# First pair of an attention-and-adapter kernel: x's mean on four column tiles, and another order of the preparation of W

## The chip, the cores and the metric

One core of one Trainium2 chip runs the whole program. The metric is the device time of one execution in microseconds (us). The engines are named PE (TensorE, matrix products), DVE (VectorE), ACT (ScalarE), POOL (GpSimd) and SP (SyncE, which here only issues DMAs).

## The reference, cut to what matters

```python
# x: (128, 128, 1024) f32, adj: (128, 128, 128) int32, W: (1, 1024, 1024), a: (1, 16, 128, 1)
h  = layernorm(x)                                    # no scale, no offset
Wh = h @ W                                           # split in 16 heads of 64
e  = leaky_relu(Wh @ a[:, :64] + Wh @ a[:, 64:], 0.2)    # one score a row and head
att = softmax(where(adj == 0, -9e15, e)) * adj
x  = x + elu(att @ Wh)
y  = layernorm(x)
gates = top-2 softmax of y[:, 0] @ router.T          # 8 experts of rank 16
x  = x + y + sum over e of gates[e] * (y @ down_e.T) @ up_e.T
```

There are 128 tiles of 128 rows and 1024 columns. W and the router, down and up tables are the same for all of them.

## The kernel before, in words

The layernorm is not applied to x. Since a row's mean drops out when W's columns have their mean taken away, the kernel centres W's columns (over the 1024 rows of W) and multiplies the product by the row's rstd afterwards. Wh's scores come out of the same product, as four extra columns beside each 256 columns of W ("score columns"), which are W times a.

Tiles are worked on in pairs q = 0 to 63. The product of two tiles with W is done as a Strassen-like scheme of seven half-sized products on blocks of W: B11, B21, B22 and the fourth block of W (loaded into the place called T1) give T3 = B22 - (fourth block), T2 = T3 + B11, T1 = B22 - T2 (which replaces the fourth block) and NT4 = B21 - T2. On x's side POOL forms four sums (`pair_sums`). Each product is 8 matmuls of 128 x 256 (260 with score columns), 16 PE instructions in the profile, since each f32 matmul shows as two. Three banks of PSUM accumulate: x (products 1 and 2), y (6, 5, 3) and z (7, 4). There are buffers for two of them at a time, so z takes the place of x once x has been read, last by DVE's `low(q, 0)`.

The order of every engine's queue is the order in which the program is written. A list `gaps` holds eight lists for each q: the work to be issued before product 1 (gap 0), between the products, and after the last one (gap 7). For q = 0 the products run in the order 1, 2, 7, 6, 5, 3, 4; for the others 1, 6, 2, 5, 7, 3, 4. Reads of a product by DVE (u2 after 6, u4 after 5, wh0 after 3, wh1 after 4) are queued where the product is issued, ahead of the next gap's work.

In the first pair W is not yet prepared, and `prepare(gaps)` spreads that work over pair 0:

- `center_x` takes the column mean from x of pair 0, so that its products 1 and 2 may use W as loaded. PE sums over 128 partitions with a matrix of 1/1024 (`mean_of`, L180), DVE subtracts (L183).
- `partial_means(h)` sums one half of W's columns, on four column tiles of PE (L191: four matmuls with 32 output rows each run side by side); ACT copies the result (L195), `column_means` (L200) adds the four parts with `sum_of` into a tile w_mean, of which `center_block` (L209) takes each block's mean away. `combine` (L746) forms T3, T2, T1 and NT4. Each is one DVE instruction over 2048 elements a partition.
- `first_stats(i)` (L306, L307 on DVE, L310 and L311 on POOL for rstd), `first_half` (L754) and `correct_p1` (L761) bring product 1's result in line with the centred W.
- `score_rows` (PE, L220) forms a times W's transpose, `center_rows` (DVE L229 to L232, ACT L235) takes its mean away, `turn_rows` (PE L244) transposes it, and `score_columns` (DVE L254 to L259) puts it beside the blocks. From pair 1 on, products read these columns.
- For pair 0 itself the scores are had another way: `score_of(b)` multiplies by a on POOL (L270), and DVE sums by head (L204).
- `high` (ACT, L442) and `low` (DVE, L446) write the attention's operands in two parts, `attention_weights` (DVE L462 to L479) the softmax, `attend` (PE L488) the product with adj, `update` (DVE L498, L506, L507, ACT L505) x + elu. `turn` and `rejoin` transpose x by DMA for the logits.
- `experts()` (L277 to L300) takes the mean off the router and down tables over their 1024 rows: for each of the two a DVE sum over 8 chunks (L281), a PE sum over partitions (L283) and a DVE subtraction (L284); then a store of the down table to DRAM (L285, SP), which later pairs gather from, and small index tables. It is issued once, in pair 1.

SP issues at the start, in this order: a, x of pair 0 transposed (1 MB), B11, B21, the two tiles of x, B22, the fourth block (about 1 MB each), W transposed (4 MB), adj, the next pair's x. SP's queue and POOL's DMA queue are in order too.

Of the kernel before, what the change touches and what calls it, by code (L numbers as in the profile page):

```python
# [8 lines left out]
F32 = mybir.dt.float32  # L9
# [5 lines left out]
ALU = mybir.AluOpType  # L15
AX = mybir.AxisListType
# [9 lines left out]
def adj_ffn_kernel(  # L26
# [16 lines left out]
    nc = tc.nc  # L43
    B, N, D = x.shape
    P = 128
    KC = D // P
    KH = KC // 2
    F = 64
    H = D // F
    ER = up_t.shape[0]  # L50
    E = router_t.shape[2]
# [3 lines left out]
    HALF = 512  # L55
# [10 lines left out]
    work = ctx.enter_context(tc.tile_pool(name="work", bufs=2))  # L66
    small = ctx.enter_context(tc.tile_pool(name="small", bufs=3))
    ps_w = ctx.enter_context(tc.tile_pool(name="ps_w", bufs=2, space=bass.MemoryType.PSUM))
    ps_m = ctx.enter_context(tc.tile_pool(name="ps_m", bufs=4, space=bass.MemoryType.PSUM))
# [7 lines left out]
    GRP = {}  # L77
# [7 lines left out]
    B11, B21, B22, T1, T2, T3, NT4 = range(7)  # L85
# [25 lines left out]
    def w_at(h, k):  # L111

        return w_sb[:, BLOCK[h][k // KH], k % KH]
# [52 lines left out]
    def spread_a():  # L166

        for h in range(NH):
# [2 lines left out]
                             start=True, stop=True)  # L171
            nc.scalar.copy(a_sum[:, h], in_two(pa))

    def center_x():

        xt = XT[0]
        px = ps_m.tile([P, HALF], F32, tag="pm", name="px")[:, 0:2 * P]
        mean = px.rearrange("p (t n) -> p t n", t=2)
        for k in range(KC):
            nc.tensor.matmul(mean, mean_of, xt[:, :, k], start=(k == 0), stop=(k == KC - 1))  # L180
        for t, lo, hi in ((0, 0, KH), (0, KH, KC), (1, 0, KC)):
            part = xt[:, t, lo:hi]
            nc.vector.tensor_tensor(part, part, mean[:, t, None].to_broadcast(part.shape),  # L183
                                    ALU.subtract)

    def partial_means(h):

        pc = ps_m.tile([P, HALF], F32, tag="pm", name="pc")
        for u in range(2):
            for c in range(KH):  # L190
                nc.tensor.matmul(pc[c * 32:(c + 1) * 32], mean_of[:, 0:32],  # L191
                                 w_sb[:, BLOCK[h][u], c, :, MAIN], start=(u == 0), stop=(u == 1),
                                 tile_position=(0, c * 32))
        part = work.tile([P, HALF], F32, tag="hp", name="part")
        nc.scalar.copy(part, pc)  # L195
        return part

    def column_means(part):
        pc = ps_m.tile([P, HALF], F32, tag="pm", name="w_mean")
# [62 lines left out]
    def score_of(b):  # L262
# [7 lines left out]
        nc.gpsimd.tensor_tensor(prod, src, a_sum[:, h], ALU.mult)  # L270
        by_head(dst, prod)

    slot = down_row = up_row = None

    def experts():

        nonlocal slot, down_row, up_row  # L277
        down_rows = down_sb.rearrange("p e r k -> p (e r) k")
        for t, n in ((router_sb.rearrange("p k e -> p e k"), E), (down_rows, ER)):
            sums = work.tile([P, ER], F32, tag="hp", name="sums")  # L280
            nc.vector.tensor_reduce(sums[:, 0:n], t, AX.X, ALU.add)  # L281
            pr = ps_m.tile([P, HALF], F32, tag="pm", name="pr")[:, 0:n]
            nc.tensor.matmul(pr, mean_of, sums[:, 0:n], start=True, stop=True)  # L283
            nc.vector.tensor_tensor(t, t, pr[:, :, None].to_broadcast([P, n, KC]), ALU.subtract)  # L284
        nc.sync.dma_start(table.rearrange("(e p) c -> p e c", p=P),  # L285
                          down_sb.rearrange("p e r k -> p e (r k)"))

# [479 lines left out]
    def prepare(gaps):  # L767

        got = {}

        def keep(name, f, *of):
            def task():
                got[name] = f(*(got.get(o, o) for o in of))
            return (task,)

        gaps[0] += [(place_a,), (spread_a,), (center_x,), (pair_sums, 0)]
        gaps[2] += [keep("part 0", partial_means, 0), (first_stats, 0),
                    keep("less", first_half), (first_stats, 1),
                    keep("", column_means, "part 0"), (keep_c11,), (high, 0, 0),
                    (combine, T3, B22, T1, ALU.subtract)]  # L780
        gaps[3] += [keep("part 1", partial_means, 1), (center_block, 0, B11),
                    keep("", correct_p1, "less"), (combine, T2, T3, B11, ALU.add), (center_block, 0, B21)]
        gaps[4] += [keep("", column_means, "part 1"), keep("rows", score_rows), (score_of, 0),
                    (center_block, 1, B22), (combine, T1, B22, T2, ALU.subtract),
                    keep("turned", center_rows, "rows")]
        gaps[5] += [(combine, NT4, B21, T2, ALU.subtract), (load_experts,)]
        gaps[6] += [keep("cols", turn_rows, "turned"), (score_of, 3)]
        gaps[7] += [keep("", score_columns, "cols"), (score_of, 1)]

    NQ = B // 2  # L790

# [1 line left out]
    for q in range(NQ + 2):  # L793
# [27 lines left out]
                gaps[3].insert(0, (turn_at_end, i + 1))  # L821
            gaps[5] += [(join, i), (join, i + 1)]
        if q + 1 < NQ:
            gaps[3 if q else 6].append((first_stats, 2 * q + 2))
            gaps[4 if q else 6] += [(pair_sums, q + 1), (first_stats, 2 * q + 3)]
        if q == NQ - 1:
            gaps[1].append((load_all,))
            gaps[5].append((order_all,))
# [15 lines left out]
                gaps[5].append((load_adj, q // 2 + 1))  # L844
        if q < NQ:
            gaps[3].insert(0, (low, q, 0))
            gaps[6] += [(low, q, 3), (low, q, 1)]

        if q + 1 < NQ:
            load_xt(q + 1)  # L850
            load_x(q + 1)
        if q == 0:
            gaps[7].append((score_of, 2))
        if q == 1:
            gaps[6].append((experts,))
        products = project(q) if q < NQ else iter(())
        for gap in gaps:
            for f, *args in gap:
# [48 lines left out]
```

## Time and profile before

| | |
|---|---|
| median of 3 runs | 1970.37 us (1970.11 to 1972.25) |
| the profiled execution | 1969.22 us, of which the profile's span is 1967.4 us |
| PE busy | 1936.3 us, 98% of the span |
| DVE busy | 1657.0 us, 84% |
| ACT / POOL busy | 1080.0 us, 55% / 835.3 us, 42% |
| mean granted PE clock | 0.994 |
| products (L373) on the chain that ended last | 77% of the span |

A row of a timeline gives the start, the length and the engine of a group of instructions on one line of the kernel, what it writes and reads, the shape of one, their number, and in brackets the time for which the engine was idle before them with what ended it. A row of busy time by stretch gives the stretch and its length, then for each engine (PE, PE's weight loads, DVE, ACT, POOL) its busy time and number of instructions, then PE's granted clock, and the share and GB/s of the DMA engines. Where PE alone is asked for, the row has PE alone. A clock of 0.50 is half speed. The records of the clock begin in this trace at 12.21 us; before that the stretches show 1.00, while matmuls of 256 columns stand 0.427 us apart there, against 0.216 later.

### The profile page before, as it was taken

What the parts mean: (1) busy time and instruction counts of PE and PEld (TensorE: products, weight loads), DVE (VectorE), ACT (ScalarE), POOL (GpSimd) and SP (SyncE); (2) the same over time, 40 slices, a digit from 0 to 9 for tenths busy, and PEclk for the clock granted to TensorE, in tenths of its full rate; (3) what the DMA queues carried; (4) which work ended last, traced back from release to release, by engine and by line L of the source; (5) the groups of instructions that cost most, each with busy time, mean ns of one, the idle gap of its engine ahead of it and who ended that gap; (6) DMA issues with size and microseconds to landing.
All of it is one profiled execution on the core that took longest, in us unless ns stands there. A gap on an engine that the chain in (4) does not pass through costs nothing.

```text
span 1967.4 us, 30167 instructions
## 1 busy us (share of the span) xinstructions
PE 1936.3 (98%) x11042; PEld 1576.6 (80%) x11042; DVE 1657.0 (84%) x3511; ACT 1080.0 (55%) x1031; POOL 835.3 (42%) x1123
## 2 busy tenths in 40 slices
PE   8799999999999999999999999999999999999997
PEld 5688888888888888888888888888888888888885
DVE  6788888888888888888888888888888888888886
ACT  1355655655555655655655655655655655555653
POOL 2344344544335544435534435534435534435530
PEclk9899999999999999999999999999999999999999
DMA  7365566565566565566566565565565565565552
GB/s 280 86 161 171 153 188 182 129 195 169 153 185 178 130 197 173 151 186 174 137 193 176 150 188 167 144 193 176 151 188 159 152 193 169 159 187 150 161 154 104
DMA packets 343671, 329.26 MB, mean 167 GB/s; under 512 B 274274, under 2 KB 276322, under 8 KB 342884
## 3 DMA queue, kind: packets, MB, share of 16 engines
q1 hardware_dynamic: 325940, 285.37, 49.4%
q0 software_dynamic: 17008, 40.91, 7.0%
q8 instruction: 88, 1.44, 0.3%
q10 hardware_dynamic: 576, 1.05, 0.1%
q14 instruction: 59, 0.48, 0.1%
HBM read 193.58 MB, written 67.63 MB: 133 GB/s over the span
## 4 chain that ended last, share of the span: by engine, by line
PE 92%; DVE 4%; DMA 1%; ACT 1%; issue 1%; POOL 0%; SPq 0%; POOLq 0%; DVEq 0%
PE pw L373 77%; PE ph L488 6%; PE pu L677 3%; PE pd L661 3%; DMA tt<-halves 1%; PE pb L624 1%; PE pl L568 1%; DVE stats L306 1%; ACT y_t L544 1%; DVE xn L506 1%; DVE xn L507 1%; DVE hp L498 0%; ACT halves L538 0%; PE pu L738 0%; DVE w_sb L746 0%
## 5 line engine op out<-in xcount | busy, mean ns | idle before, releaser
L373 PE MATMUL pw<-w_sb,xt 128*128 128x260 f32 (+1 forms) x4096 | 951.8, 387 | 7.0 <-issue 5.6
L373 PEld LDWEIGHTS pw<-w_sb,xt 128*128 128x128 f32 x4096 | 770.5, 191 | 154.3 <-issue 34.4
L373 PE MATMUL pw<-w_sb,s 128*128 128x260 f32 (+1 forms) x3072 | 711.1, 385 | 2.9 <-DVE w_sb L746 2.0
L373 PEld LDWEIGHTS pw<-w_sb,s 128*128 128x128 f32 x3072 | 578.0, 190 | 117.1 <-issue 21.0
L310 POOL TENSOR_SCALAR rstd<-mv 128x2 f32<-128x2 f32 x128 | 30.4, 238 | 862.7 <-DVE mv L307 857.4
L544 ACT COPY y_t<-tt 128x2048 uint16<-128x2048 uint16 x126 | 315.8, 2509 | 77.0 <-DMA tt<-halves 76.6
L306 DVE BATCH_NORM_STATS2 stats<-xn 128x6 f32<-128x512 f32 x512 | 324.0, 675 | 0.1
L642 POOL DMA_INDIRECT down<-table,at_down x248 | 252.0, 1016 | 163.7 <-DVE e L462 89.3
L538 ACT COPY halves<-xn 128x2048 uint16<-128x2048 uint16 x126 | 239.7, 1902 | 120.6 <-DVE xn L507 76.9
L442 ACT ACTIVATE parts<-wh,rstd 128x512 fp32r<-128x512 f32 x192 | 133.6, 715 | 224.9 <-DVE wh L381 224.6
L505 ACT ACTIVATE ex<-hp 128x1024 f32<-128x1024 f32 x128 | 135.4, 1058 | 179.3 <-DVE hp L498 177.6
L681 DVE SCALAR_TENSOR_TENSOR xn<-pu,rstd,xn 128x512 f32<-128x512 f32 x248 | 169.0, 745 | 21.8 <-PE pu L677 21.8
L498 DVE TENSOR_TENSOR hp<-ph,att 128x512 f32<-128x512 f32 x256 | 161.4, 672 | 10.6 <-PE ph L488 10.1
L507 DVE SCALAR_TENSOR_TENSOR xn<-ex,xn 128x1024 f32<-128x1024 f32 x128 | 156.8, 1225 | 13.7 <-issue 0.5
L488 PE MATMUL ph<-parts,adj_f 128*128 128x512 f32 x512 | 164.2, 442 | 1.3 <-ACT parts L442 0.9
L506 DVE SCALAR_TENSOR_TENSOR xn<-hp,xn 128x1024 f32<-128x1024 f32 x128 | 156.8, 1225 | 4.4
L560 ACT ACTIVATE xn<-xn,off,mul 128x1024 f32<-128x1024 f32 x128 | 151.2, 1230 | 0.7 <-POOL off L525 0.7
L446 DVE SCALAR_TENSOR_TENSOR parts<-wh,rstd,parts 128x512 fp32r<-128x512 f32 x192 | 139.1, 752 | 12.4 <-ACT parts L442 12.4
L381 DVE TENSOR_TENSOR wh<-pw,u 128x520 f32<-128x520 f32 (+1 forms) x128 | 89.3, 698 | 54.7 <-PE pw L373 51.3
L381 DVE TENSOR_TENSOR wh<-pw,p 128x520 f32<-128x520 f32 (+1 forms) x64 | 44.8, 700 | 81.4 <-PE pw L373 81.4
L488 PEld LDWEIGHTS ph<-parts,adj_f 128*128 128x128 f32 x512 | 96.5, 189 | 20.3 <-ACT parts L442 1.2
L311 POOL TENSOR_TENSOR rstd<-rstd,half_pow 128x2 f32<-128x2 f32 x128 | 91.3, 713 | 10.7
(138 smaller groups left out, 1473.5 us busy)
## 6 DMA issues: line engine op xcount, KB each, us to landing
xt<-in_x_t SPq DMA_DIRECT2D x128, 512.0 KB
xn<-in_x SPq DMA_DIRECT2D x128, 512.0 KB
out_y<-xn SPq DMA_DIRECT2D x124, 512.0 KB
adj_f<-in_adj_t POOLq DMA_DIRECT2D x32, 256.0 KB
adj_i<-in_adj SPq DMA_DIRECT2D x32, 256.0 KB
w_sb<-in_w SPq DMA_DIRECT2D x4, 1040.0 KB
down<-table,at_down POOLq DMA_INDIRECT x248
wt_sb<-in_w_t SPq DMA_DIRECT2D x1, 2048.0 KB
```

What stands on the lines that cost most here:

```text
L306: nc.vector.bn_stats(st[:, h, :], X[i][:, h * HALF:(h + 1) * HALF])
L373: nc.tensor.matmul(dst[:, j, cols], lhs[:, k, :], w_sb[:, rhs, k, j, cols], start=(first and k == 0), stop=(k == KH - 1), skip_group_check ...
L446: nc.vector.scalar_tensor_tensor(in_two(PARTS[q][:, 1, b]), block, rstd, in_two(PARTS[q][:, 0, b].bitcast(F32)), op0=ALU.mult, op1=ALU.sub ...
L488: nc.tensor.matmul(PH[i][h], GRP[g]["adj_f"][:, t, :], PARTS[q][:, s, NH * (i % 2) + h], start=(s == 0), stop=(s == 1))
L498: nc.vector.tensor_tensor(hp[:, h * HALF:(h + 1) * HALF].rearrange("p (h f) -> p h f", f=F), ph.rearrange("p (h f) -> p h f", f=F), att[:, ...
L506: nc.vector.scalar_tensor_tensor(xt, hp, 0.0, xt, op0=ALU.max, op1=ALU.add)
L507: nc.vector.scalar_tensor_tensor(xt, ex, 1.0, xt, op0=ALU.min, op1=ALU.add)
L538: nc.scalar.copy(halves, X[i].bitcast(U16).rearrange("p (d s) -> p s d", s=2))
L544: nc.scalar.copy(y_of(i).bitcast(U16).rearrange("p k (n s) -> p s k n", s=2), TT.pop(i).rearrange("p (s k) n -> p s k n", s=2))
L560: nc.scalar.activation(X[i], X[i], AF.Identity, bias=GRP[g]["off"][:, t:t + 1], scale=GRP[g]["mul"][:, t:t + 1])
L642: nc.gpsimd.indirect_dma_start(out=st["down"][:, j * R:(j + 1) * R].rearrange("p r k -> p (r k)"), out_offset=None, in_=table, in_offset=b ...
L681: nc.vector.scalar_tensor_tensor(y[:, cols], pu[t], st["rstd"][:, t:t + 1], y[:, cols], op0=ALU.mult, op1=ALU.add)
```

## The change

`center_x` takes its mean in the way of `partial_means`: eight matmuls on four column tiles, a copy by ACT, and one matmul that adds the four parts (function `fourths`, used for both). `partial_means(0)` moves to before product 2. In gap 2 the column mean and T3 come ahead of the first statistics; the second column mean moves from gap 4 to gap 3, the centring of B21 from gap 3 to gap 4, the transposes of the score rows from gap 6 to gap 5, the score columns from gap 7 to gap 6. All four `score_of` of pair 0, and two of its `low`, are issued in gap 7. The statistics of tiles 2 and 3 move from pair 0's gap 6 to pair 1's gap 2, ahead of tile 1's update. The tables' sums over chunks (`over_chunks`) are issued in pair 1's gap 5, and `experts`, now with one matmul for both tables, moves from its gap 6 to its gap 7.

```diff
+    def fourths(rows):
+        n = rows[0].free_size()
+        pc = ps_m.tile([P, HALF], F32, tag="pm", name="pc")[:, 0:n]
+        for u in range(2):
+            for c in range(KH):
+                nc.tensor.matmul(pc[c * 32:(c + 1) * 32], mean_of[:, 0:32], rows[u * KH + c],
+                                 start=(u == 0), stop=(u == 1), tile_position=(0, c * 32))
+        part = work.tile([P, HALF], F32, tag="hp", name="part")[:, 0:n]
+        nc.scalar.copy(part, pc)
+        return part
+
     def center_x():
         xt = XT[0]
+        part = fourths([xt[:, :, k] for k in range(KC)])
         px = ps_m.tile([P, HALF], F32, tag="pm", name="px")[:, 0:2 * P]
+        nc.tensor.matmul(px, sum_of, part, start=True, stop=True)
         mean = px.rearrange("p (t n) -> p t n", t=2)
-        for k in range(KC):
-            nc.tensor.matmul(mean, mean_of, xt[:, :, k], start=(k == 0), stop=(k == KC - 1))
...
     def partial_means(h):
...
+        return fourths([w_at(h, k)[:, :, MAIN] for k in range(KC)])
...
+    def over_chunks():
+        sums = small.tile([P, E + ER], F32, tag="sums", name="sums", bufs=1)
+        nc.vector.tensor_reduce(sums[:, 0:E], router_sb.rearrange("p k e -> p e k"), AX.X, ALU.add)
+        nc.vector.tensor_reduce(sums[:, E:], down_sb.rearrange("p e r k -> p (e r) k"), AX.X,
+                                ALU.add)
+        GRP["sums"] = sums
...
     def experts():
-        for t, n in ((router_sb.rearrange("p k e -> p e k"), E), (down_rows, ER)):
-            sums = work.tile([P, ER], F32, tag="hp", name="sums")
-            nc.vector.tensor_reduce(sums[:, 0:n], t, AX.X, ALU.add)
-            pr = ps_m.tile([P, HALF], F32, tag="pm", name="pr")[:, 0:n]
-            nc.tensor.matmul(pr, mean_of, sums[:, 0:n], start=True, stop=True)
-            nc.vector.tensor_tensor(t, t, pr[:, :, None].to_broadcast([P, n, KC]), ALU.subtract)
+        pr = ps_m.tile([P, HALF], F32, tag="pm", name="pr")
+        nc.tensor.matmul(pr[:, 0:E + ER], mean_of, GRP["sums"], start=True, stop=True)
+        for t, lo, n in ((router_sb.rearrange("p k e -> p e k"), 0, E),
+                         (down_sb.rearrange("p e r k -> p (e r) k"), E, ER)):
+            nc.vector.tensor_tensor(t, t, pr[:, lo:lo + n, None].to_broadcast([P, n, KC]),
+                                    ALU.subtract)
...
         gaps[0] += [(place_a,), (spread_a,), (center_x,), (pair_sums, 0)]
-        gaps[2] += [keep("part 0", partial_means, 0), (first_stats, 0),
-                    keep("less", first_half), (first_stats, 1),
-                    keep("", column_means, "part 0"), (keep_c11,), (high, 0, 0),
-                    (combine, T3, B22, T1, ALU.subtract)]
-        gaps[3] += [keep("part 1", partial_means, 1), (center_block, 0, B11),
-                    keep("", correct_p1, "less"), (combine, T2, T3, B11, ALU.add), (center_block, 0, B21)]
-        gaps[4] += [keep("", column_means, "part 1"), keep("rows", score_rows), (score_of, 0),
-                    (center_block, 1, B22), (combine, T1, B22, T2, ALU.subtract),
+        gaps[1] += [keep("part 0", partial_means, 0)]
+        gaps[2] += [keep("", column_means, "part 0"), (keep_c11,),
+                    (combine, T3, B22, T1, ALU.subtract), (first_stats, 0),
+                    keep("less", first_half), (first_stats, 1), (high, 0, 0)]
+        gaps[3] += [keep("part 1", partial_means, 1), keep("", column_means, "part 1"),
+                    (center_block, 0, B11), keep("", correct_p1, "less"),
+                    (combine, T2, T3, B11, ALU.add)]
+        gaps[4] += [keep("rows", score_rows), (center_block, 1, B22),
+                    (combine, T1, B22, T2, ALU.subtract), (center_block, 0, B21),
                     keep("turned", center_rows, "rows")]
-        gaps[5] += [(combine, NT4, B21, T2, ALU.subtract), (load_experts,)]
-        gaps[6] += [keep("cols", turn_rows, "turned"), (score_of, 3)]
-        gaps[7] += [keep("", score_columns, "cols"), (score_of, 1)]
+        gaps[5] += [keep("cols", turn_rows, "turned"), (combine, NT4, B21, T2, ALU.subtract),
+                    (load_experts,)]
+        gaps[6] += [keep("", score_columns, "cols")]
...
         if q + 1 < NQ:
-            gaps[3 if q else 6].append((first_stats, 2 * q + 2))
-            gaps[4 if q else 6] += [(pair_sums, q + 1), (first_stats, 2 * q + 3)]
+            if q:
+                gaps[3].append((first_stats, 2 * q + 2))
+            gaps[4 if q else 6].append((pair_sums, q + 1))
+            if q:
+                gaps[4].append((first_stats, 2 * q + 3))
...
-            gaps[6] += [(low, q, 3), (low, q, 1)]
+            gaps[6 if q else 7] += [(low, q, 3), (low, q, 1)]
...
         if q == 0:
-            gaps[7].append((score_of, 2))
+            gaps[7] += [(score_of, 0), (score_of, 3), (score_of, 1), (score_of, 2)]
         if q == 1:
-            gaps[6].append((experts,))
+            gaps[2][2:2] = [(first_stats, 2), (first_stats, 3)]
+            gaps[5].append((over_chunks,))
+            gaps[7].append((experts,))
```

## The prediction

> **What bounds the kernel now.** I read the page's busy times first, then the busy times by stretch, to see where TensorE (PE) is not full.
>
> ```profile
> PE 1936.3 (98%) x11042; PEld 1576.6 (80%) x11042; DVE 1657.0 (84%) x3511; ACT 1080.0 (55%) x1031; POOL 835.3 (42%) x1123
> 0.00:100.00 100.00, 79.47 (x340) 58.40 (x341) 67.12 (x123) 25.21 (x28) 30.23 (x40) 0.91 0.50 181
> 100.00:1930.00 1830.00, 1829.62 (x10576) 1499.22 (x10578) 1562.69 (x3331) 1044.25 (x991) 803.60 (x1078) 1.00 0.58 168
> ```
>
> From 100 to 1930 us PE is idle for 0.4 us in all. All that this change touches lies in the first 100 us, where PE is idle for 20.5 us and its clock is at 0.91. A microsecond won or lost by the time the third pair runs stays won or lost to the end. So I went through PE's timeline up to there, then VectorE's (DVE), GpSimd's (POOL) and SP's.
>
> ```profile
> 7.23 6.14 PE L180 MATMUL px<-xt,mean_of 128*128 128x256 f32 x16 [0.97 <-DMA xt<-in_x_t]
> 18.55 3.72 PE L373 MATMUL pw<-w_sb,xt 128*128 128x256 f32 x16 [0.68 <-ACT p L395]
> 22.20 1.93 PE L191 MATMUL pc<-w_sb,mean_of 128*32 128x512 f32 x16
> 31.85 3.69 PE L373 MATMUL pw<-w_sb,s 128*128 128x256 f32 x16 [0.57 <-DVE w_sb L746]
> 41.43 3.72 PE L373 MATMUL pw<-w_sb,s 128*128 128x256 f32 x16 [1.47 <-DVE w_sb L746]
> 59.62 5.61 PE L373 MATMUL pw<-w_sb,xt 128*128 128x260 f32 x16 [5.57 <-issue]
> 77.44 3.67 PE L373 MATMUL pw<-w_sb,xt 128*128 128x260 f32 x16
> 89.53 0.59 PE L283 MATMUL pr<-sums,mean_of 128*128 128x8 f32 x2 [4.91 <-DVE sums L281]
> 92.20 9.82 PE L373 MATMUL pw<-w_sb,xt 128*128 128x260 f32 x32
> ```
>
> These are the start, the length and the idle time before. The two big holes are 5.57 us ahead of pair 1's product 1 (it waits for the score columns, written by DVE at 59.36) and 4.91 + 1.49 us ahead of the tables' sums. After each hole the products run at half clock (5.61 us instead of 3.67; 9.82 for two instead of 7.2). The change aims at both holes. What takes their place is decided by DVE:
>
> ```profile
> 19.91 3.23 DVE L746 TENSOR_TENSOR w_sb<-w_sb 128x2048 f32<-128x2048 f32 x1
> 25.90 0.75 DVE L446 SCALAR_TENSOR_TENSOR parts<-pw,rstd,parts 128x512 fp32r<-128x512 f32 x1 [2.75 <-ACT parts L442]
> 29.42 2.28 DVE L746 TENSOR_TENSOR w_sb<-w_sb 128x2048 f32<-128x2048 f32 x1
> 76.17 0.74 DVE L446 SCALAR_TENSOR_TENSOR parts<-pw,rstd,parts 128x512 fp32r<-128x512 f32 x1
> 17.16 2.83 SPq L102 DMA_DIRECT2D xt<-in_x_t  x2
> ```
>
> They are T3, low(0,0), T2, low(1,0), and two loads on SP's queue. SP's waits put each of those loads behind a transfer of w_sb; the second left at 19.67, so W's last block (T1) landed at about 19.65. T3 reads that block.
>
> **Part by part.** Times are of the profiled execution (span 1967.4, 1969.22 in all; the median of the runs is 1970.37, 1.15 above it).
>
> *x's mean.* Sixteen instructions, 0.427 us apart at half clock, took 6.15 us. On four column tiles, four run at once: L191's sixteen of 512 columns take 1.93 at full clock; half the columns at half clock is about the same, 2.1, to 9.35. ACT's copy is bounded by 0.26 (64 wide, L469) and 0.58 (512 wide); I take 0.4. L200's two matmuls (1.12) at half the columns and half clock are 1.1. The mean is there at 11.1 instead of 13.38, product 1 starts at 11.85 instead of 14.16. But the clock rises at 12.21 in this trace, and all its later changes (56.58, 63.41, 87.30, 97.54) lie a multiple of 3.413 us from that. With the new pauses the stretch 8.80 to 12.21 is half idle, so I take the next edge, 15.62: product 1 does 8.8 instructions at 0.427 and 7.2 at 0.216, and ends at 17.4 against 17.89.
>
> *Column means earlier.* Part 0 (1.93) covers the 0.68 that product 2 waits for ACT, and the 0.71 before the first column mean is gone. Product 2 runs 19.1 to 22.6, product 7 from 23.45 (25.80 before): 2.35 us ahead.
>
> *T3 ahead of the first statistics.* Here the lead is lost. DVE is through with x at 13.2, and T3, now at the head of its queue, waits for T1's block until 19.7. Behind it stand statistics 0, the half sum and statistics 1 (15.75 to 19.91: 4.16 us), which ran in that time before. T3 ends at 21.95 (2.28, as L746 takes when POOL is idle; POOL's pair sums now end at 18.9), statistics at 26.1; POOL's rstd 1.0 (78.44 to 79.45), ACT's high 0.70, then low 0.75 to 28.75, the centring of B11 2.2, p1's correction 0.66, T2 2.2: 33.85. Product 6 starts at 33.9, not 31.85: **+2.05**, after 3.3 us without work.
>
> *The clock at that hole.* In 29.28 to 32.69 PE has only the second column mean, 1.12 (L200's row) of 3.41 us, 33%. By the rows of PE's busy time in such stretches:
>
> ```profile
> 39.52:42.93 3.41, 1.95 (x14) 1.00 0.00 0
> 53.17:56.58 3.41, 0.88 (x5) 1.00 0.49 124
> 83.89:87.30 3.41, 0.73 (x4) 1.00 0.00 0
> 1944.14:1947.55 3.41, 1.45 (x14) 1.00 0.00 0
> ```
>
> The last three (26, 21, 42%) were followed by half clock, the first (57%) was not; 33% lies with the three. So I take half clock from 32.69 on. It ends at 39.52, the first edge after a full stretch (60.00 to 63.41 was such a one): 13 instructions of product 6 at 0.427, three at 0.216, to 40.4 instead of 37.5, **+2.9**. The Trainium skill ("TensorE: Matmul & The Clock Gate", the table of Why this matters for your kernels) asks for an idle gap of over about 3 us before the clock halves, in Part 1 for a whole idle window; by that rule product 6 would run at full clock and the sum below would be 2.9 lower. The trace does not agree: in the second row the clock halved at 56.58, 2.5 us after PE's last work, which ended at 54.05.
>
> *The middle of pair 0.* After product 6 DVE reads u2 (0.69), centres B22 and makes T1 (2.2 each): product 5 at 45.7 (41.43). Then B21 (2.2) and the score rows (1.75), ACT's two (1.26), the transposes (0.9), now ahead of product 3: 51.9 (46.03). Product 4 runs 55.4 to 59.0 (54.05): **+4.9**. Score columns are out at 56.4, so pair 1's product 1 needs no wait and no half clock: 58.9 to 62.5, against 65.2: **-2.7**. The hole of 5.57 is paid for by three smaller ones.
>
> *Scores and statistics.* POOL gets n after DVE at 54.3 (49.95): 0.9 for three small steps, 0.7 for a DMA, 5.3 for the pair sums, then all four score products, 5.05: 66.3. The last head sum is at 67.0 (63.77). So attention weights, update 0 and u2's read come 3.2 late, u2 at 74.2; pair 1's product 5 starts at 74.3 (73.94). Then DVE has statistics 0 (1.43), the moved statistics of tiles 2 and 3 (2.87), update 1 (3.74) and low(1,0) (0.74): 83.0 instead of 76.91. Product 7 needs the bank that low(1,0) reads: **83.0 against 77.44**, 4.9 us of idling after product 5, so half clock again, 5.9 long. Product 3 ends at 92.5 (84.6).
>
> *Tables.* Product 4 follows at once, 92.3 (92.20), at full clock; the one remaining matmul of the tables is 0.3 instead of 0.59 + 0.79. The two chunk sums (0.26 + 1.21) lie where DVE waits for product 3. The table's store moves from 93.7 to 98.4 on SP's queue; behind it are the loads that left at 98.58 before. If that cover were gone, pair sums at 116 still have 17 us. Attention of tile 2 starts at 99.6 (101.67): **-2.1**. Logits then wait 0.8 for ACT's rejoin. Pair 3's product 1 comes at 124.7 instead of 125.98: **-1.3**.
>
> *One unknown.* In 42.93 to 46.34 PE has 0.99 of the score rows and 0.61 of product 5, 47%, between the 42% that halved and the 57% that did not. If it halves, product 5 ends 1.8 later, DVE's chain up to low(1,0) comes 1.6 later, and product 7 runs at half clock throughout (6.8): 2.5 in all, **+1.2**. I take the middle, no change: 1970.4. Further bounds: T3 beside POOL costs 3.23 (+1.0). The grid of edges need not lie the same in other runs: half clock that lasts one stretch of 3.41 more or less is 1.7 either way.
>
> **Rivals.**
> *Faster: product 6 keeps its clock.* Everything up to low(1,0) then comes 2.9 earlier: -1.3 - 2.9 = -4.2, so 1966.2. For it: no stretch of 33% is in the trace. Against: 42% halved. If the landing of T1's block did not hold DVE at all, nearly all would go that the two holes cost (5.57 + 1.9 + 4.91 + 1.49 + 2.6, some 16 us, 1954); the load that left at 19.67 speaks against that. Together 0.20.
> *Slower: PE loses its clock at product 5 as well, and for a stretch longer.* It decides once a stretch of 3.41 us holds under about half of PE's work. Its price: +1.2, 1.7 for the longer stretch and 1.0 for T3, +3.9: 1974.3. For it: the three holes that the sum puts in place of one are each 1.7 to 5 long. Against: the first row above. 0.27.
> *DVE's backlog gives more back in pair 2.* Its low(2,0) ends at about 112.1, just as product 5 ends there; before it ended at 112.95, 1.3 before product 7. It costs 0 to 1, within no change.
>
> **How the numbers follow.** A measurement of this kernel can tell about 0.2% (3.9 us) from no change. The forecast (-3.9 to +3.9) gets 0.53, faster 0.20, slower 0.27. The range takes in the two rivals and the bound of T3 and of the grid: 1964.5 to 1976.0; the forecast's own is 1966.5 to 1974.3.
>
> **What would show it.** In the changed profile: a DVE wait of 6 us before L746's first, ended by a transfer of w_sb; PE idle for about 3.3 us before product 6, then 0.427 us between its instructions; no wait before pair 1's product 1; a hole of 5 us before pair 1's product 7; none before product 4. If T3 starts before 19 us, or product 6 before 32, or product 7 before 78, the sum is wrong and the kernel faster.

## The result, and the profile after

The changed kernel took 1970.58 us (median of 4 runs, 1969.87 to 1971.52), the kernel before 1970.25 beside it (4 runs, 1970.11 to 1972.25). The ratio is 1.000, with a 95% interval of 0.9982 to 1.0017: no change that can be measured. The profiled execution took 1970.70 us, with a span of 1968.8.

That is not because little happened. First the busy time by stretch, as shown of before; the columns after the length are PE, PE's weight loads, DVE, ACT and POOL, then PE's clock:

```profile
0.00:100.00 100.00, 80.61 (x349) 57.29 (x349) 68.23 (x123) 25.76 (x29) 27.81 (x40) 0.95 0.49 176
100.00:1930.00 1830.00, 1828.52 (x10572) 1499.05 (x10570) 1559.88 (x3332) 1045.55 (x991) 803.84 (x1078) 1.00 0.59 168
```

PE's idle time in the first 100 us went from 20.5 to 19.4 us, its clock from 0.91 to 0.95. Where the holes lie now is in PE's timeline (start, length, then in brackets the idle time before and what ended it):

```profile
7.46 1.93 PE L180 MATMUL pc<-xt,mean_of 128*32 128x256 f32 x16 [1.18 <-DMA xt<-in_x_t]
11.88 6.30 PE L383 MATMUL pw<-w_sb,xt 128*128 128x256 f32 x16 [0.78 <-DVE xt L195]
33.72 5.38 PE L383 MATMUL pw<-w_sb,s 128*128 128x256 f32 x16 [1.98 <-DVE w_sb L756]
44.41 3.72 PE L383 MATMUL pw<-w_sb,s 128*128 128x256 f32 x16 [1.73 <-DVE w_sb L756]
53.49 7.12 PE L383 MATMUL pw<-w_sb,xt 128*128 128x256 f32 x32
82.90 6.68 PE L383 MATMUL pw<-w_sb,xt 128*128 128x260 f32 x16 [4.85 <-DVE parts L456]
92.92 3.67 PE L383 MATMUL pw<-w_sb,xt 128*128 128x260 f32 x16
96.43 0.40 PE L290 MATMUL pr<-sums,mean_of 128*128 128x136 f32 x2
```

Both of the old holes are gone: pair 1's product 1 follows product 4 without a wait and at full clock (the row of 32 holds both), and the tables' one matmul (L290) waits for nothing. But product 6 of pair 0 (33.72) comes after a new hole and runs at half clock at first, and product 7 of pair 1 (82.90) comes after another of 4.85 us and is 6.68 long. DVE's timeline has the reasons, T3, T2, the four additions that make the score columns, and low(1,0):

```profile
19.98 2.29 DVE L756 TENSOR_TENSOR w_sb<-w_sb 128x2048 f32<-128x2048 f32 x1 [6.43 <-DMA w_sb<-in_w]
31.30 2.28 DVE L756 TENSOR_TENSOR w_sb<-w_sb 128x2048 f32<-128x2048 f32 x1
55.06 0.81 DVE L259 TENSOR_TENSOR w_sb<-w_sb,b 128x32 f32<-128x32 f32 x1
55.91 3.74 DVE L262 TENSOR_TENSOR w_sb<-w_sb 128x32 f32<-128x32 f32 x3
82.10 0.75 DVE L456 SCALAR_TENSOR_TENSOR parts<-pw,rstd,parts 128x512 fp32r<-128x512 f32 x1
```

**How far a lead goes.** To compare kernels I take, besides the time, the lead: by how much the logits of pair 3 begin earlier than before. They begin at 121.43 us before and at 120.83 after, a lead of 0.60. At the next to last logits (1898.05 before, 1897.58 after) the lead is still 0.47; over 1777 us it moved by 0.13. Then it is swallowed by the end of the program, where PE waits again and again and its clock halves. The last sixteen matmuls, before and after:

```profile
1956.08 7.11 PE L738 MATMUL pu<-w_sb,dn_all 128*128 128x512 f32 x16 [1.03 <-issue]
```

```profile
1955.81 8.85 PE L748 MATMUL pu<-w_sb,dn_all 128*128 128x512 f32 x16 [1.03 <-issue]
```

The granted clock was at half in the end stretch from 1947.6 to 1954.4 before, and from 1949.1 to 1959.3 after: there it reached into these matmuls. From the last logits to PE's last work it is 13.8 us before and 16.3 after; in the kernels below it is 14.1 to 17.6, without any of them changing that code. So a single execution is uncertain by up to almost 4 us for this reason. Between the two logits named, the lead of the kernels below moved by 0.7 at most.

### The profile page after: what moved, and what is told of

It is laid out like the page before. It is cut to its first block, busy times and chain, and to the rows that moved or that the text cites. A ratio compares the mean times of both kernels' runs of the same rounds, so it can differ in the third digit from the quotient of the medians.

```text
span 1968.8 us, 30168 instructions
## 1 busy us (share of the span) xinstructions
PE 1937.1 (98%) x11042; PEld 1575.5 (80%) x11042; DVE 1654.9 (84%) x3511; ACT 1080.4 (55%) x1032; POOL 833.1 (42%) x1123
## 4 chain that ended last, share of the span: by engine, by line
PE 91%; DVE 5%; DMA 2%; ACT 1%; issue 0%; POOL 0%; SPq 0%; DVEq 0%; POOLq 0%; ACTq 0%
PE pw L383 76%; PE ph L498 6%; PE pu L687 3%; PE pd L671 3%; DMA tt<-halves 1%; PE pb L634 1%; PE pl L578 1%; DVE stats L316 1%; DMA w_sb<-in_w 1%; ACT y_t L554 1%; DVE xn L516 1%; DVE hp L508 1%; DVE xn L517 1%; ACT halves L548 0%; PE pu L748 0%
```

## The experiments

All but the change itself (4 runs) were timed in 5 to 11 runs each, beside runs of the kernel before (medians 1970.1 to 1970.3). The lead is from each one's profiled execution, one of those runs.

| kernel | median, us | ratio to before, 95% interval | lead at pair 3, us |
|---|---|---|---|
| the change | 1970.58 | 1.0000, 0.9982 to 1.0017 | 0.60 |
| a1_T3_behind_stats | 1965.93 | 0.9979, 0.9969 to 0.9988 | 5.57 |
| a2_block_before_x | 1967.26 | 0.9986, 0.9977 to 0.9995 | 5.36 |
| a3_stats_back | 1970.99 | 1.0000, 0.9991 to 1.0009 | 1.03 |
| a4_mean_full_width | 1970.49 | 1.0002, 0.9993 to 1.0011 | -1.29 |
| a5_stats_in_wait | 1967.15 | 0.9984, 0.9975 to 0.9993 | 4.82 |
| b1_tables_alone | 1963.54 | 0.9965, 0.9951 to 0.9979 | 7.78 |
| b2_tables_and_columns | 1966.19 | 0.9978, 0.9969 to 0.9987 | 5.81 |
| c1_combined | 1963.80 | 0.9970, 0.9959 to 0.9981 | 7.44 |
| d1_sums_early | 1962.26 | 0.9959, 0.9945 to 0.9972 | 8.24 |
| d2_columns_sums_early | 1961.43 | 0.9957, 0.9943 to 0.9971 | 7.74 |
| d3_sums_early_weights_first | 1962.38 | 0.9959, 0.9945 to 0.9972 | 8.79 |

**One part of the change undone (a1 to a4), or put elsewhere (a5).** First T3's place in DVE's queue:

```diff
-                    (combine, T3, B22, T1, ALU.subtract), (first_stats, 0),
-                    keep("less", first_half), (first_stats, 1), (high, 0, 0)]
+                    (first_stats, 0), keep("less", first_half), (first_stats, 1),
+                    (high, 0, 0), (combine, T3, B22, T1, ALU.subtract)]
```

> The changed kernel with T3 behind the first statistics again (DVE's order in gap 2 of the first pair; all else as changed). My theory (T3, waiting for W's last block at the head of DVE's queue, holds the statistics and so T2): DVE does the statistics from 13.6 to 17.8, T3 still starts at about 20.0, low(0,0) at 25.1 instead of 27.8, T2 ends at 30.9 instead of 33.5, product 6 of pair 0 starts at about 31.7 instead of 33.7 without a hole of 2 us and at full clock, and ends at 35.2 instead of 39.0. All of that chain up to product 7 of pair 1 comes 3.8 earlier (79.1 instead of 82.9); the time is 3 to 4 us below the changed kernel, some 1966.8. Rival (the start does not matter, since pair 1's DVE backlog or POOL's score products set the end): product 6 is earlier but product 7 of pair 1 stays at 82 to 83 and the time at 1970.

The theory held. PE's timeline of this kernel:

```profile
30.66 3.62 PE L383 MATMUL pw<-w_sb,s 128*128 128x256 f32 x16
78.12 6.49 PE L383 MATMUL pw<-w_sb,xt 128*128 128x260 f32 x16 [4.85 <-DVE parts L456]
```

Product 6 starts 3.06 us earlier, with no hole ahead of it and at full clock. T3 itself starts at 19.84, no later than in the change (19.98): the block's landing holds it either way, and the statistics now run in the wait instead of behind it. Product 7 of pair 1 keeps its hole of 4.85 and its half clock, 4.8 us earlier. The order of one queue entry is worth 4.65 us by the medians and 4.97 by the lead; the ten runs (1964.05 to 1967.62) and the four of the change (1969.87 to 1971.52) do not overlap.

The other end of the same wait is the transfer. Here SP loads W's last two blocks ahead of x's tiles:

```diff
-        if i == 2:
-            load_x(0)
         nc.sync.dma_start(w_sb[:, b], w[:, i])
+    load_x(0)
```

> The changed kernel with SP's loads in another order: B22 and W's last block before the two tiles of x, so the block that T3 reads lands at about 17.3 instead of 19.8, and x at 18.6 and 19.9 instead of 13.6 and 14.9. My theory: T3 starts when the block lands, 17.4. POOL's pair sums run until 18.7, so T3 takes 2.3 to 3.2; statistics end at 23.8 to 24.8 instead of 25.9, T2 at 31.4 to 32.4 instead of 33.5, and the time falls by 1 to 3 us (the hole before product 6 is shorter, and less of it runs at half clock). Rival: DVE's wait at 13.5 is not for that block; T3 stays at 20 and nothing moves.

The rows are T3 and product 6:

```profile
17.48 2.29 DVE L755 TENSOR_TENSOR w_sb<-w_sb 128x2048 f32<-128x2048 f32 x1 [3.88 <-DMA w_sb<-in_w]
31.23 3.69 PE L382 MATMUL pw<-w_sb,s 128*128 128x256 f32 x16 [0.31 <-DVE w_sb L755]
```

T3 starts when the block lands, 2.5 us earlier, product 6 at 31.23 after 0.31 us, and the lead is 5.36, as with a1. The time falls by 3.3 us, a little more than expected. So it is the wait of T3 for the fourth block that counts, whichever of its ends is moved.

The statistics of tiles 2 and 3, put back where they were before:

```diff
-            if q:
-                gaps[3].append((first_stats, 2 * q + 2))
-            gaps[4 if q else 6].append((pair_sums, q + 1))
-            if q:
-                gaps[4].append((first_stats, 2 * q + 3))
+            gaps[3 if q else 6].append((first_stats, 2 * q + 2))
+            gaps[4 if q else 6] += [(pair_sums, q + 1), (first_stats, 2 * q + 3)]
...
-            gaps[2][2:2] = [(first_stats, 2), (first_stats, 3)]
```

> The changed kernel with the statistics of tiles 2 and 3 back in pair 0's gap 6 (as before the change). My theory (they lie between tile 0's update and low(1,0), and so make the hole before product 7 of pair 1): update 1 and low(1,0) move forward by 2.9, but the lows of pair 0 and the head sums move back by up to 1.5; low(1,0) ends at about 81 instead of 82.85, product 7 starts at 81 instead of 82.9, the time falls by 1.5 to 2 us. Rival (the lows of pair 0 hold attend 0, and so products 6 and 2 of pair 1): product 6 of pair 1 starts at 66 instead of 63.4, and the time stays or rises by 1.

By the median the rival held. In PE's timeline the hole before product 7 (second row) is cut from 4.85 to 2.11, but the statistics now stand ahead of two of pair 0's lows, and attention waits 4.16 us for these (first row), where it waited 1.80 in the change:

```profile
66.66 0.54 PE L498 MATMUL ph<-parts,adj_f 128*128 128x512 f32 x1 [4.16 <-DVE parts L456]
84.16 3.74 PE L383 MATMUL pw<-w_sb,xt 128*128 128x260 f32 x16 [2.11 <-issue]
```

So moving them was no gain and no loss by the median: 2.9 us of DVE's work on its critical stretch is late in either place. A small gain of the old place is not excluded: the eleven runs fall in two groups, five at 1967.0 to 1969.0 and six at 1971.0 to 1972.1, and the profiled one, of the second group, lost 1.3 us at product 6 of pair 0 (6.69 long, against 5.38 in the change) to the clock. Off that stretch the statistics hold nothing. In the next kernel they stand in gap 3, while DVE waits for product 6:

```diff
-                    (combine, T2, T3, B11, ALU.add)]
+                    (combine, T2, T3, B11, ALU.add), (first_stats, 2), (first_stats, 3)]
...
-            gaps[2][2:2] = [(first_stats, 2), (first_stats, 3)]
```

> The changed kernel with the statistics of tiles 2 and 3 behind T2 in pair 0's gap 3, where DVE waits for product 6 (33.5 to 39.1), instead of ahead of tile 1's update. x of these tiles lands at 34.3 and 35.6. My theory (they make the hole before product 7 of pair 1): they end at 37.3 without holding anything, low(1,0) ends 2.9 earlier (80.0 instead of 82.85), product 7 starts at 80.0, the hole is 2 instead of 4.85 us and the half clock behind it (3 us) goes: the time falls by 3 to 5.5 us, to some 1965 to 1967.5. Rival (a bank or ACT holds product 7, not low(1,0)): product 7 stays at 82 to 83 and the time within 1 us of 1970.5.

The theory held in the time and in the place of product 7:

```profile
80.11 5.43 PE L383 MATMUL pw<-w_sb,xt 128*128 128x260 f32 x16 [2.11 <-issue]
```

The time is 3.4 us less than the change's, and the hole 2.11 instead of 4.85. Only the half clock behind it did not go: the product is still 5.43 long.

x's mean as before, in sixteen full-width matmuls, the rest of the change kept:

```diff
-        part = fourths([xt[:, :, k] for k in range(KC)])
...
-        nc.tensor.matmul(px, sum_of, part, start=True, stop=True)
...
+        for k in range(KC):
+            nc.tensor.matmul(mean, mean_of, xt[:, :, k], start=(k == 0), stop=(k == KC - 1))
```

> The changed kernel with x's mean taken as before (eight matmuls of full width, no copy; all else as changed). My theory (the earlier start is given away at DVE's wait for W's last block): product 1 starts at about 14.1 instead of 11.9 and ends at 17.9, but T3 still starts at 20.0, T2 ends at 33.5 and product 6 starts at 33.7, so the time is the changed kernel's within 1 us, about 1970.5. Rival (four column tiles are worth the 2.3 us by which they end earlier): the time rises by about 2 us, to 1972.5.

No difference in the median. Product 1 starts at 14.43 instead of 11.88, but ends at 18.15, against 18.18 with the four column tiles: what the mean gains, half clock takes. T3 is another matter, and the expectation left it out:

```profile
20.16 3.27 DVE L756 TENSOR_TENSOR w_sb<-w_sb 128x2048 f32<-128x2048 f32 x1 [4.07 <-DMA w_sb<-in_w]
```

It starts as late as in the change (19.98) but takes 3.27 instead of 2.29, since POOL's pair sums, which follow x's mean, now end at 21.29 and not at 18.70. So the profiled execution has product 6 at 34.88, 1.2 later, and 6.0 long, and its lead is 1.9 smaller. It is also the slowest of eleven runs (1968.1 to 1972.6): the column tiles' mean may be worth a microsecond by T3, which these runs are too scattered to show.

**One part alone (b1, b2).** The kernel before with only the tables' part: both chunk sums in gap 5 of pair 1, one matmul, `experts` in gap 7.

```diff
...
         if q == 1:
-            gaps[6].append((experts,))
+            gaps[5].append((over_chunks,))
+            gaps[7].append((experts,))
```

> The kernel before with the tables' part of the change alone: sums over chunks in pair 1's gap 5, one matmul, and the tables' subtraction in gap 7. My theory: the holes of 4.91 and 1.49 and the half clock behind them go, product 4 of pair 1 starts at 84.6 instead of 92.2 and pair 2 some 9 to 10 earlier; of that DVE's low(2,0) gives back 1 to 2 before product 7 of pair 2. The time falls by 7 to 9 us, to some 1962 to 1963: this part alone is worth more than the whole change. Rival (what comes next, DVE's and ACT's work for tiles 2 and 3, holds pair 2 as long as the hole did): the time falls by less than 3 us.

This part alone is worth 6.7 us (4.1 to 9.7 by its interval), just under what was expected. PE's timeline, from the hole that stays to the tables' matmul:

```profile
59.99 5.39 PE L380 MATMUL pw<-w_sb,xt 128*128 128x260 f32 x16 [5.56 <-issue]
84.60 3.67 PE L380 MATMUL pw<-w_sb,xt 128*128 128x260 f32 x16
88.10 0.40 PE L287 MATMUL pr<-sums,mean_of 128*128 128x136 f32 x2
```

Product 4 of pair 1 starts at 84.60 at full clock; it stood at 92.20 before. So the change holds one edit worth 6.7 and others that, by difference, cost 7.0 together.

b2 adds to b1 that the score columns come first in gap 6, so that pair 1's product 1 has no hole:

```diff
-        gaps[6] += [keep("cols", turn_rows, "turned"), (score_of, 3)]
-        gaps[7] += [keep("", score_columns, "cols"), (score_of, 1)]
+        gaps[6] += [keep("cols", turn_rows, "turned"), keep("", score_columns, "cols"),
+                    (score_of, 3)]
+        gaps[7] += [(score_of, 1)]
```

> The kernel before with the tables' part, as in the run of the tables alone, and the score columns ahead of the other work of gap 6. My theory (DVE and POOL, not the score columns, set pair 1: the attention weights of pair 0 wait for POOL's last score product at 62.2): the hole of 5.56 before pair 1's product 1 goes, product 1 runs at 54.2 to 57.8 instead of 60.0 to 65.2; but the attention weights still start at 63.8, u2 is read at 71, product 5 of pair 1 starts at 71 to 72 instead of 74.1 and product 7 at 76.9 to 77.5 as before. The time falls by 0 to 1.5 us against the tables alone (1963.5). Rival (the hole of 5.56 is what it costs): the time falls by 5 to 7 us, to 1957.

My expectation was wrong in sign: 2.7 slower than b1, the lead 2.0 smaller. Product 1 did move into the hole: it follows product 4 without a wait, both in one row from 49.91 to 57.04. What failed is the price of the score columns. DVE's and POOL's timelines, and PE's row of attention:

```profile
50.72 2.87 DVE L256 TENSOR_TENSOR w_sb<-w_sb,b 128x32 f32<-128x32 f32 x1
53.63 3.76 DVE L259 TENSOR_TENSOR w_sb<-w_sb 128x32 f32<-128x32 f32 x3
57.31 0.67 DVE L204 TENSOR_REDUCE wh<-prod 128x8 f32<-128x512 f32 x1
```

```profile
51.04 1.28 POOL L270 TENSOR_TENSOR prod<-wh,a_sum 128x512 f32<-128x512 f32 x1
52.26 1.27 POOL L336 TENSOR_TENSOR s<-xt 128x512 f32<-128x512 f32 x1
53.61 1.27 POOL L337 TENSOR_TENSOR s<-s,xt 128x512 f32<-128x512 f32 x1
```

```profile
62.14 0.70 PE L495 MATMUL ph<-parts,adj_f 128*128 128x512 f32 x1 [4.41 <-DVE parts L453]
```

Four additions of 32 elements a partition take 6.6 us. The first ends at 53.59, when POOL's second operation has ended (53.53); the other three end 0.05 us after each of POOL's next three. The lows behind them then end at 62.09, attention waits 4.41 us for them, and the clock halves.

**The faults put right together (c1).** The change with T3 behind the statistics, the statistics of tile 2 in gap 4 and of tile 3 in gap 7, three of the four score products issued earlier on POOL (`score_of` is split in two for the fourth), B21's centring back in gap 3, and the last two lows of pair 0 in the other order:

```diff
-        gaps[2] += [keep("", column_means, "part 0"), (keep_c11,),
-                    (combine, T3, B22, T1, ALU.subtract), (first_stats, 0),
-                    keep("less", first_half), (first_stats, 1), (high, 0, 0)]
+        gaps[2] += [keep("", column_means, "part 0"), (keep_c11,), (first_stats, 0),
+                    keep("less", first_half), (first_stats, 1), (high, 0, 0),
+                    (combine, T3, B22, T1, ALU.subtract)]
...
+                    (combine, T2, T3, B11, ALU.add), (center_block, 0, B21), (score_of, 0)]
...
+                    keep("turned", center_rows, "rows"), (first_stats, 2)]
...
+                    (score_of, 3), (load_experts,)]
-        gaps[6] += [keep("", score_columns, "cols")]
+        gaps[6] += [keep("", score_columns, "cols"), (score_of, 1)]
...
-            gaps[7] += [(score_of, 0), (score_of, 3), (score_of, 1), (score_of, 2)]
+            gaps[7] += [(score_mul, 2), (first_stats, 3), (score_sum, 2)]
...
-            gaps[2][2:2] = [(first_stats, 2), (first_stats, 3)]
```

> The changed kernel with: T3 behind the first statistics; B21 centred behind T2 in gap 3, while DVE waits for product 6; score product 0 there too, score product 3 in gap 5, score product 1 ahead of the pair sums, so that POOL has one of four left at the end; statistics of tile 2 behind the score rows' sums in gap 4, of tile 3 behind pair 0's last low; low(0,1) ahead of low(0,3). My theory (DVE's and POOL's chain to the attention weights of pair 0, then to low(1,0), is what the whole start hangs on): T2 at 29.9, product 6 at 30.7, product 3 at 44.2, product 1 of pair 1 at 51 to 52, attention weights at 58 to 59 instead of 67, u2 at 65, product 7 of pair 1 at 71 to 72 instead of 82.9 with a hole under 2 us. The time falls by 10 to 13 us below the changed kernel: 1957.5 to 1960.5, below both and below the tables alone. Rival (something later, ACT's rejoin and the DMA transposes of pair 1, is the next bound): 1963 to 1965, as the tables alone.

The theory's time was missed; c1 is as fast as b1, no faster. That is the rival's time, but its reason is not shown: the chain was already 6 us late at product 7 of pair 1. The additions and the first instruction of the attention weights:

```profile
51.95 2.98 DVE L259 TENSOR_TENSOR w_sb<-w_sb,b 128x32 f32<-128x32 f32 x1
54.97 3.75 DVE L262 TENSOR_TENSOR w_sb<-w_sb 128x32 f32<-128x32 f32 x3
64.28 0.18 DVE L479 SCALAR_TENSOR_TENSOR e<-wh 128x24 f32<-128x24 f32 x1
```

The weights started at 64.28 instead of 58 to 59, and product 7 of pair 1 at 77.45 instead of 71 to 72. The four additions again took 6.8 us (51.95 to 58.72) beside POOL's work; d1 below tests how much of the delay is theirs.

**POOL's sums away from the additions (d1 to d3).** They move from gap 6 to gap 5, where POOL is idle in b2 and has one score product in c1: d2 is b2 with this move, d1 and d3 are c1 with it. The diff is d2's; in c1 the same entry goes ahead of `(score_of, 3)`.

```diff
-        gaps[5] += [(combine, NT4, B21, T2, ALU.subtract), (load_experts,)]
+        gaps[5] += [(combine, NT4, B21, T2, ALU.subtract), (pair_sums, 1), (load_experts,)]
...
-            gaps[4 if q else 6] += [(pair_sums, q + 1), (first_stats, 2 * q + 3)]
+            if q:
+                gaps[4].append((pair_sums, q + 1))
+            gaps[4 if q else 6].append((first_stats, 2 * q + 3))
```

> The kernel of before with the tables' part and the score columns first in gap 6, which missed its forecast (1966.2 against 1963.5 with the tables alone), now with the second pair's four row sums on POOL moved to gap 5. Theory: the miss was the additions held up beside POOL's sums, 6.7 us for four. They fall under 2.5 us, the lows of tiles 0's second half end about 2.5 earlier (59.6 instead of 62.1), the attention weights start at about 63.5 instead of 65.9, and the time is 1963 to 1964.5, 2 to 3 less than without the move. Rival: the miss came from the order of VectorE's work alone (columns ahead of the head sums and lows): 1965.5 to 1967.

The theory held in its mechanism. DVE's timeline of d2, the same four additions, and PE's row of attention:

```profile
52.03 0.41 DVE L256 TENSOR_TENSOR w_sb<-w_sb,b 128x32 f32<-128x32 f32 x1
52.48 0.52 DVE L259 TENSOR_TENSOR w_sb<-w_sb 128x32 f32<-128x32 f32 x3
```

```profile
60.35 0.50 PE L495 MATMUL ph<-parts,adj_f 128*128 128x512 f32 x1 [2.29 <-DVE parts L453]
```

The four take 0.93 us instead of 6.63. The lows end 1.8 earlier, attention waits 2.29 instead of 4.41, the clock stays full from 40 to 100 us. The lead grows by 1.9, and the time falls by 4.8; the difference is the program's end, which in the two profiled executions is 14.1 and 17.6 us long. Of this gain in the time, then, some 2 us are shown to come from the move. It also answers b2's question: pair 1's product 1 now has no hole, and yet the lead (7.74) is that of b1 (7.78), which keeps the hole of 5.56. By the lead, closing that hole was worth nothing.

> Combined kernel, with only the second pair's four row sums on POOL moved forward, from gap 6 (52.4 to 58.7 us, beside the score columns) to gap 5, ahead of POOL's own score product, where POOL has been idle. Theory: VectorE's 128x32 additions (0.19 us each when POOL is quiet) cost 2.98, 1.31, 1.19 and 1.30 in the combined kernel because each ends only when POOL's running two-input operation ends, so the four cost 6.8 where 0.8 is their own. With the sums gone from there, at most the one or two score products stand beside them: the four take under 2.5 us together, the attention weights start at 60 to 61 instead of 64.3, product 7 of pair 1 at 73.5 to 75.5 instead of 77.45, and the time is 1960 to 1962 (against 1963.8). Rival: the additions are slow in themselves or for another reason, or the place lost to the chip's clock returns elsewhere: additions still over 5 us, time 1963 to 1965.

The additions fell to 2.28 us, as the theory has it; the weights did not start at 60 to 61 but at 63.66, the time is 0.3 above its range. Two rows say why:

```profile
52.75 0.69 DVE L207 TENSOR_REDUCE wh<-prod 128x8 f32<-128x512 f32 x1 [4.84 <-POOL prod L273]
55.26 5.13 PE L390 MATMUL pw<-w_sb,xt 128*128 128x260 f32 x16 [2.99 <-issue]
```

POOL's score product now stood behind the sums, DVE waited 4.84 us for it, and pair 1's product 1 behind that started at 55.26 after a hole of 2.99. The stall was traded for a wait.

d3 has the statistics of tile 3 behind the attention weights as well:

```diff
-            gaps[7] += [(score_mul, 2), (first_stats, 3), (score_sum, 2)]
+            gaps[7].append((score_of, 2))
         if q == 1:
+            gaps[0].append((first_stats, 3))
```

> As d1_sums_early, and the statistics of tile 3 (1.45 us of VectorE) moved from ahead of the last head sum to behind the attention weights. Theory: the attention weights are the chain that ends last in this stretch, so they start 1.4 us earlier than in d1_sums_early, at 58.5 to 60, product 7 of pair 1 moves by 0.5 to 1.4, time 1958.5 to 1961.5, 0.5 to 1.4 under d1_sums_early. Rival: the wait that ends last before product 7 is then the statistics of tiles 2 and 3 and their low parts, and nothing is gained: within 0.5 of d1_sums_early.

The weights start 1.75 earlier than in d1, at 61.91 (58.5 to 60 expected), but product 7 only 0.56 (76.26): its product 5 now came after a hole of 2.29 and ran at half clock (5.46). The time is the same as d1's, as the rival had it.

d2 is the fastest median, 1961.43, against 1970.11 of before in the same rounds. By the leads (7.74 and 7.78) and the overlapping intervals it is not shown to beat b1, which needs the tables' edit alone.

## Why the prediction was right, point by point

The forecast was 1970.4 and no change; it came to 1970.58. The path that the sum describes is in the main the one that the trace shows, but that the two agree within 0.2 us is in part luck: errors in both directions met, as the points below say, and executions of the same code differ by more than that.

- *The two old holes.* Right: both gone, at full clock.
- *x's mean.* Sized too well. Product 1 ended at 18.18, not 17.4: the clock rose at 17.14, not at 15.62, and twelve of its sixteen instructions ran at half. Product 7 came at 24.38 instead of 23.45. It did not matter, because the next step waits for the fourth block: in a4 product 7 comes at 24.35, after a mean taken at full width.
- *T3's wait.* Right, and the step that decides: DVE waited 6.43 us (6 said), until 19.98 (19.7), low(0,0) ended at 28.52 (28.75), T2 at 33.58 (33.85), product 6 started at 33.72 (33.9). The hole just before it was 1.98 us, not 3.3, since the second column mean came later too. a1 and a2 show that this wait costs 3.3 to 4.7 us in the end.
- *The clock at product 6.* Right that it halves, too long by one stretch of 3.41. Three stretches of the trace after: one in which PE had work for 42%, the next, and the one ahead of product 5:

```profile
30.80:34.21 3.41, 1.43 (x4) 0.60 (x5) 2.78 (x2) 0.00 (x0) 0.00 (x0) 1.00 1.03 410
34.21:37.62 3.41, 3.41 (x9) 2.66 (x8) 0.00 (x0) 0.00 (x0) 0.00 (x0) 0.50 0.66 258
41.03:44.44 3.41, 1.68 (x17) 0.30 (x9) 3.38 (x3) 0.00 (x0) 0.00 (x0) 1.00 0.00 0
```

  The half clock lasted from 34.21 to 37.62 and cost 1.7, where 2.9 was put down. The reason is the grid, the fixed step of 3.413 us at which the clock changes: its edges stand 0.07 us past a multiple of 3.413 in this execution and 1.97 past one in that of before, which the prediction named as a bound. The Trainium skill ("TensorE: Matmul & The Clock Gate", Part 1) calls the window free-running; the traces agree, with these two offsets. The demand of the same page (the table of Why this matters for your kernels) for an idle gap of over about 3 us does not fit here either: the clock halved at 34.21 after a gap of 1.98. With the 3.3 us that the prediction expected, the table's rule would have halved the clock too; only by Part 1's whole idle window would product 6 have kept it.
- *The one unknown.* The third row: 49% of work ahead of product 5, and the clock stayed full. The slower rival, which lived from that, did not come. The prediction's own sum for this case was a gain of 1.3, not no change. The share of work, by which the prediction judged such stretches, does not decide alone: 1.60 us of PE's work in 3.41 kept the clock in a1 (56.35 to 59.76), 1.59 lost it in a2 (56.37 to 59.78), and 1.42 kept it in a3 (80.63 to 84.04).
- *The middle of pair 0.* Product 5 at 44.41 (45.7), product 3 at 50.03 (51.9), product 1 of pair 1 done at 60.61 (62.5): 1.3 to 1.9 early, mostly by the clock.
- *Scores and statistics.* Right in its result for a reason the sum did not have. The last head sum ended at 66.94 (67.0), product 5 of pair 1 started at 74.28 (74.3), low(1,0) ended at 82.85 (83.0), product 7 started at 82.90 (83.0). But I had POOL's chain as the late one, and it started 1.4 early and then waited 1.22 for DVE. What took the early start back were the additions of the score columns, 4.55 us beside POOL's sums against 2.43 before. So two errors of the sum, 1.3 to 1.9 us too much for the clock and 2.1 too little for DVE, met in the same number. The additions before, and POOL's wait after (those after stand in DVE's timeline above):

```profile
60.12 0.91 DVE L256 TENSOR_TENSOR w_sb<-w_sb,b 128x32 f32<-128x32 f32 x1
61.06 1.52 DVE L259 TENSOR_TENSOR w_sb<-w_sb 128x32 f32<-128x32 f32 x3
```

```profile
63.72 2.49 POOL L273 TENSOR_TENSOR prod<-wh,a_sum 128x512 f32<-128x512 f32 x2 [1.22 <-DVE sc L207]
```

- *Tables, and the end.* Product 4 at 92.92 (92.3), attention at 99.98 (99.6), logits 1.06 late (0.8), pair 3's product 1 at 125.37 (124.7): a gain of 0.6, not 1.3, since the half clock at product 7 cost 0.8 more than put down. The profiled executions' ends then took 2.5 us more after than before, which the sum could not know.

The gain that the change aimed at is thus found. Of the tables' 6.7 us nothing was left: T3's place gives back 4.65 (a1), and the statistics, ahead of tile 1's update, 3.4 against a place in DVE's wait (a5), though their old place is no better (a3). The two are not simply added: c1, which mends both and moves more besides, gets back 6.8 and is no faster than b1. What sets the length of the program's end in one execution, beyond the place of its clock's edges, stays open.

## What to carry to other kernels

When an instruction is moved to the head of an in-order queue, look at what its inputs wait for: T3 waited for a transfer that arrived no earlier, and everything that had filled the wait went behind it. A hole on the bounding engine is worth its length only if the chain behind it is also early: the hole of 4.91 and 1.49 us at the tables was worth 6.7, the one of 5.56 before pair 1's product 1 nothing by the lead (d2 against b1). And a kernel's parts should be timed alone: this change was one edit worth 6.7 us and several that cost 7.0, by difference.

## What the runs showed of the hardware

DVE and POOL hold each other up, by far more than I had expected. A DVE addition with two operands in SBUF, 0.19 us long when POOL has no two-operand work (the last three in d2), took 0.8 to 3.0 us while POOL ran its 128x512 two-operand operations in the change, b2 and c1, and ended about 0.05 us after one of them had. The other way round, in d2 POOL's subtraction beside DVE's 2048-wide NT4 took 3.36 instead of 1.27 while NT4 kept its 2.28:

```profile
46.34 2.28 DVE L753 TENSOR_TENSOR w_sb<-w_sb 128x2048 f32<-128x2048 f32 x1
46.40 3.36 POOL L337 TENSOR_TENSOR s<-s,xt 128x512 f32<-128x512 f32 x1
```

DVE's head sums, with one operand, kept their 0.67 to 0.69 beside POOL's score products (the change, at 63.57 and 65.02). The Trainium skill ("GPSIMD Engine Reference", 1. Specifications) says that POOL's SBUF interfaces are shared with VectorE, with contention at DVE instructions of two SBUF inputs; the rows agree, and give its size: whole instructions of the other engine, one in most rows and two at the first addition of b2 and of c1, not a share of the speed.
